# Layer 0 of a four-layer graph network: the last 20 nodes' softmax weights turned by TensorE, the first batch ahead of older values, and the output weights loaded from ScalarE's queue

## The chip, the cores and the metric

The kernel runs on one core of a Trainium2 chip. A core has five engines with a queue of instructions each: TensorE (PE; its weight loads are listed apart as PEld), VectorE (DVE), ScalarE (ACT), GpSimd (POOL) and SyncE (SP, which here issues transfers only). 16 DMA engines move the data. The metric is the device time of one execution in microseconds; the time of a kernel is the median over several runs.

## The reference

x is 2708 x 512, adj is 2708 x 2708, all f32. Four residual layers follow one another, each ended by a layer norm. The change touches the end of layer 0, which is attention over the graph with 8 heads of key width 64:

```python
keys = jnp.einsum('nj,hjk->hnk', node_matrix, Wks)
queries = jnp.einsum('nj,hjk->hnk', node_matrix, Wqs)
values = jnp.einsum('nj,hjk->hnk', node_matrix, Wvs)
atts = jnp.einsum('hqk,hmk->hqm', queries, keys) / key_dim ** 0.5
atts = atts - 1e+16 * (1.0 - adj)[None, :, :]
atts = jax.nn.softmax(atts, axis=-1)
return jnp.einsum('hqm,hmk,hko->qo', atts, values, Wo)
...
x = _layernorm(x + _L0_gnn_ref(x, adj, ...), axis=-1)
```

Layers 1 to 3 (a two-step linear layer with a normalised adjacency, a one-head graph attention, and a normalised graph convolution) come after it and are not touched.

## The kernel before

**Tiling.** The 2708 nodes are 22 chunks of 128 rows; the last, chunk 21 (`LAST`), has 20 rows. For queries, layer 0 works on items: one chunk and one pair of heads (j is the head in the pair, p the pair). There are 84 such items of class `Pair`, and one more of class `Last`, which packs all four pairs of the 20-row chunk into one item: query rows 32p to 32p+31 of its tiles belong to pair p, and of those the ones from `FILL` = 12 on are the 20 real ones.

**One item.** The nodes attended to are cut into three batches, chunks 0-7, 8-15 and 16-21 (`ends` = 0, 8, 16, 22; `ND` = 16).
- `scores` (L408): PE multiplies queries with keys into PSUM tiles pss (pool `ps_s`, tags s0 and s1 with two banks each); DVE adds the mask and keeps the row maximum (L421).
- `weights(k)` (L438): ACT takes the exponential of batch k in place, in tile s, and sums it (L443).
- The values need these weights with the attended nodes on the partitions, so each 128x128 block must be transposed. For the batches 0 and 1 that is done in two steps: `blocks` (L445) transposes blocks of 32x32 on DVE into a tile d (L450; one instruction of 128x1024 for each head), and `deal` (L455) moves groups of 32 partitions into a tile e with four transfers of 256 KB from SP's queue (L460).
- `turn` (L466): batch 2 is transposed on PE against the identity (L479 to L488, tiles pst), and ACT copies it out (L480, L489, L490; tiles pt, pt2, lastT).
- `values` (L514; for `Last` L555): PE sums V times the weights (L506) into av, for `Last` into four banks avz of `ps_s`, which take the order batch 2, 0, 1. At the end ACT copies av to ot (L526; `Last`: four copies into otz, L570), and POOL stores it in a DRAM tensor otd (L527, L571).

Pools: s 5 buffers, d 2, e 3, av 1.

**The loop.** Iteration i starts the scores of item i (`new`) while `cur` (item i-1) is turned into weights, and `late` and `old` (items i-2 and i-3) take their values. Under `manual_schedule` PE, DVE and ACT execute in the order in which the loop writes their instructions; SP's and POOL's order is made by the scheduler. In iteration 85 there is no new item: `cur` is the `Last` item, `late` the pair 3 of chunk 20, and `old` its pair 2, of which the values of nodes 8-15 are still to do. In iteration 86 `Last` takes its own values. Between, `heads_sums` (L575) reduces the row sums of the exponentials and takes reciprocals, and `heads_rows` (L588) transposes them on PE (prs), copies them on ACT (rst, L594) and stores them in DRAM as rs_d (L595, by POOL). `last_sums` (L597) does the same for the 20 rows (prz, rstz L605, rz_d L606). rst and rstz share one buffer.

**The po stage.** From L751 on, outside the manual order, each chunk c loads its heads from otd (otl, L753) and x (L754), loads the reciprocals broadcast over partitions (rb, L762, two transfers from rs_d, for the last chunk rz_d), multiplies on POOL (L763), multiplies with the output weights wo_sb on PE (po, L766, four matmuls a chunk), adds x on DVE (L767) and applies the layer norm. otl and rb have three buffers each. wo_sb (1 MB) is loaded ahead by `load_rows` (L112), which issues from SP at L113. The PSUM banks of po belong to a pool that is opened after the loop and takes over the banks of pst, av and the `ps_s` tiles.

Of the kernel before, what the change touches and what calls it, by code (L numbers as in the profile page):

```python
# [8 lines left out]
F32 = mybir.dt.float32  # L9
AF = mybir.ActivationFunctionType  # L10
# [5 lines left out]
P = 128  # L16
BLK = 512
# [5 lines left out]
def kernel(  # L23
# [22 lines left out]
    nc = tc.nc  # L46
# [11 lines left out]
    def cols(b):  # L58
        return b * BLK, min(BLK, N - b * BLK)
# [11 lines left out]
    ident = const.tile([P, P], F32, tag="ident", name="ident")  # L71
# [40 lines left out]
    def load_rows(t, src):  # L112
        nc.sync.dma_start(t, src.rearrange("(k p) f -> p k f", p=P))  # L113
# [3 lines left out]
    ends = [0, 8, 16, NC]  # L117
    ND = ends[2]
    KD4 = P // 32
# [16 lines left out]
    FILL = 32 - LR  # L136
    otd = [dram.tile([P, NP, rows(c)[1]], F32, tag=f"otd{c}", name=f"otd{c}") for c in range(NC)]
    with ExitStack() as l0:
# [12 lines left out]
        def batch(k):  # L151

            n0 = ends[k] * P
            return n0, min(ends[k + 1] * P, N) - n0
# [24 lines left out]
        def row_sums(c, k):  # L179

            r0, q = rows(c)
            a = loaded[c][0]
            n0, w = batch(k)
            dst = dgp[:, c, k : k + 1]
            if c == LAST:
                q, dst = 32, dgz[:, k : k + 1]
            nc.scalar.activation(a[:q, n0 : n0 + w], a[:q, n0 : n0 + w], AF.Copy, accum_out=dst[:q])  # L187
            if c == LAST and k == NW - 1:
                nc.sync.dma_start(dgp[:LR, c, :], dgz[FILL:32, :])
# [13 lines left out]
        def mask(c, k):  # L203

            n0, w = batch(k)
            a = loaded[c][0][:, n0 : n0 + w]
            nc.scalar.activation(a, a, AF.Identity, scale=1e16, bias=far)

        with tc.tile_pool(name="kvw", bufs=1) as kvw, tc.tile_pool(name="xTb", bufs=2) as xtp, tc.tile_pool(
            name="ps_0", bufs=8, space=PSUM  # L210
# [52 lines left out]
            for b in order:  # L263
                n0, w = cols(b)
# [108 lines left out]
        ps_s = l0.enter_context(tc.tile_pool(name="ps_s", bufs=2, space=PSUM, reuse_waits="tile"))  # L373
        sp = l0.enter_context(tc.tile_pool(name="sp", bufs=5, reuse_waits="tile"))
        dp = l0.enter_context(tc.tile_pool(name="dp", bufs=2, reuse_waits="tile"))
        ep = l0.enter_context(tc.tile_pool(name="ep", bufs=3, reuse_waits="tile"))
        ptp = l0.enter_context(tc.tile_pool(name="ptp", bufs=1, reuse_waits="tile"))

        class Pair:
# [58 lines left out]
            def weights(self, k):  # L438

                w = batch(k)[1]  # L440
                for j in range(2):
                    s = self.s[k][:, j, :w]
                    nc.scalar.activation(s, s, AF.Exp, bias=self.nm[j], accum_out=self.sums(j, k))  # L443

            def blocks(self, k, j):  # L445

                n = ends[k + 1] - ends[k]
                if k not in self.D:
                    self.D[k] = dp.tile([P, KD4, 2, n, 32], F32, tag="d", name=f"d{self.c}_{self.p}_{k}")
                nc.vector.transpose(  # L450
                    self.D[k][:, :, j].rearrange("p i m x -> p m i x"),
                    self.s[k][:, j, : n * P].rearrange("p (m i x) -> p m i x", i=KD4, x=32),
                )

            def deal(self, k):  # L455

                n = ends[k + 1] - ends[k]
                e = ep.tile([P, KD4, 2, n, 32], F32, tag="e", name=f"e{self.c}_{self.p}_{k}")
                for g in range(KD4):
                    nc.sync.dma_start(  # L460
                        e[:, g].rearrange("p j m x -> p (j m x)"),
                        self.D[k][32 * g : 32 * g + 32].rearrange("p i j m x -> p i (j m x)"),
                    )
                self.E[ends[k]] = e
# [30 lines left out]
            def weight(self, m, j):  # L495

                if m >= ND:
                    return self.pts[m, j]
                f = max(f for f in self.E if f <= m)
                return self.E[f][:, :, j, m - f, :]  # L500
# [28 lines left out]
        class Last(Pair):  # L529
# [19 lines left out]
            def weight(self, m, p, j):  # L549
                if m >= ND:  # L550
                    return self.pts[m, j][:, 32 * p + FILL : 32 * p + 32]
                f = max(f for f in self.E if f <= m)
                return self.E[f][:, p, j, m - f, FILL:]

            def values(self, m0, m1):  # L555
                if self.done == 0:
# [52 lines left out]
        items = [(c, p) for c in range(LAST) for p in range(NP)] + [(LAST, 0)]  # L609
        old = late = cur = None  # L610
        with tc.manual_schedule(
            engines={mybir.EngineType.PE, mybir.EngineType.DVE, mybir.EngineType.Activation}
        ):
            for i in range(len(items) + 3):
                new = None
                prep = i < len(items) and items[i][0] < LAST and items[i][1] > 0
                if cur is not None:
                    cur.weights(0)
                if i < len(items):
                    c, p = items[i]  # L620
                    if c + 1 < NC:
                        load_chunk(c + 1, p)
                    new = (Pair if c < LAST else Last)(c, p)
                    new.scores(0, 0)
                    new.scores(0, 1)
                if old is not None:
                    old.values(ends[1], ND)
                if prep:
                    row_sums(c + 1, p - 1)
                if cur is not None:  # L630
                    cur.weights(1)
                    cur.blocks(0, 0)
                    cur.blocks(0, 1)
                    cur.deal(0)
                if prep:
                    loops(c + 1, p - 1)
                if new is not None:
                    new.scores(1, 0)
                    new.scores(1, 1)
                if cur is not None:  # L640
                    cur.weights(2)
                if late is not None:
                    late.values(ND, NC)
                    late.values(0, ends[1])
                if cur is not None:
                    cur.blocks(1, 0)
                    cur.blocks(1, 1)
                    cur.deal(1)
                if prep:
                    mask(c + 1, p - 1)  # L650
                if new is not None:
                    new.scores(2, 0)
                    new.scores(2, 1)
                    new.maxima()
                if i in (HALF0 * NP + 2, len(items)):
                    sums = heads_sums(i == len(items))
                if cur is not None:
                    cur.turn()
                if i in (HALF0 * NP + 3, len(items) + 1):
                    heads_rows(*sums)  # L660
                if i == len(items) + 1:
                    last_sums()
                old, late, cur = late, cur, new
# [82 lines left out]

    with tc.tile_pool(name="wo", bufs=1, reuse_waits="tile") as wop:
        wo_sb = wop.tile([P, KC, D], F32, tag="wo", name="wo_sb")
        load_rows(wo_sb, wo)
        for c in range(NC):  # L750
            r0, q = rows(c)  # L751
            ot = wop.tile([P, NP, P], F32, tag="ot", name=f"otl{c}", bufs=3)
            nc.sync.dma_start(ot[:, :, :q], otd[c])  # L753
            nc.sync.dma_start(X[c][:q], x[r0 : r0 + q, :])  # L754
            rb = wop.tile([P, NP, P], F32, tag="rb", name=f"rb{c}", bufs=3)
            heads = rz_d if c == LAST else rs_d[c >= HALF0][c % HALF0]
            heads = heads.rearrange("j p q -> j (p q)")
            for j in range(2):
                dst = rb[j * KD : (j + 1) * KD]
                dst = dst[:, :, :q] if c == LAST else dst.rearrange("k p q -> k (p q)")  # L760
                src = rz_d[j, :, FILL:] if c == LAST else heads[j]
                nc.sync.dma_start(dst, src.partition_broadcast(KD))  # L762
            nc.gpsimd.tensor_tensor(ot[:, :, :q], ot[:, :, :q], rb[:, :, :q], ALU.mult)  # L763
            po = ps_acc.tile([P, BLK], F32, tag="acc", name=f"po{c}")
            for p in range(NP):
                nc.tensor.matmul(po[:q, :], ot[:, p, :q], wo_sb[:, p, :], start=(p == 0), stop=(p == NP - 1))  # L766
            nc.vector.tensor_tensor(X[c][:q], po[:q, :], X[c][:q], ALU.add)  # L767
            layernorm(X[c][:q], X[c][:q], q)
# [118 lines left out]
    if True:  # L887
# [115 lines left out]
        for b in range(NB):  # L1003
            for m, _ in enumerate(graph1(b)):
# [6 lines left out]
                if b == NB - 2 and m in (3, 7, 11, 15):  # L1011
                    c = first[(m - 3) // 4]
                    top0(c, 0, piece(c, 0))
                if b == NB - 1 and m < len(first):
                    c = first[m]
# [79 lines left out]
    if True:  # L1095
# [53 lines left out]
        for b in range(NB):  # L1149
            if b:  # L1150
                queue = Maxima(b + 1) if b + 1 < NB else None
            for m in graph2(b):
                if m % 4 == 2 and 0 <= m // 4 < len(chunks_of(b)) and b:
                    c = chunks_of(b)[m // 4]
# [25 lines left out]
    with tc.tile_pool(name="zp", bufs=2) as zp:  # L1180
# [87 lines left out]
        w = cols(TAIL)[1]  # L1268
# [22 lines left out]
        while n0 < NH * P:  # L1291
            w = min(BLK, NH * P - n0)
            n1 = NH * P + n0
            nchunks = w // P
            j = n0 // BLK
# [26 lines left out]
            m4, m7, e = banks(f"m4_{j}"), banks(f"m7_{j}"), banks(f"e0_{j}")  # L1322
# [13 lines left out]
            m3, m6, e = banks(f"m3_{j}"), banks(f"m6_{j}"), banks(f"e1_{j}")  # L1336
# [61 lines left out]
```

## Time and profile before

| | us |
|---|---|
| median of 3 runs | 2578.68 (2576.52 to 2579.57) |
| the profiled execution | 2579.97 |
| its span, from first to last instruction | 2578.2 |
| PE busy in it | 2515.9 |
| first scores' exponential of the `Last` item (L443) | starts 1216.91 |
| last values of the `Last` item on PE (L506) | end 1242.79 |
| first matmul of the po stage (L766) | starts 1245.40 |

The mean granted clock of PE over the span is 0.993 of full speed. In the profile each group of instructions is named by its line, engine and operation with the tiles that it writes and reads. An idle time in brackets is that of the engine before the instruction, with what ended it; "issue" there means that the profile shows nothing that was waited for. A wait for several things is put down to the one that came last. The engines' order around the change matters more than their totals: an instruction that waits holds up all that stands behind it in its engine's queue.

### The profile page before, as it was taken

How to read it: one execution, taken by the hardware profiler on the slowest of the kernel's cores; microseconds unless marked ns; L12 is line 12 of the kernel's file. 1: busy time of each engine (PE TensorE's matmuls, PEld its weight loads, DVE VectorE, ACT ScalarE, POOL GpSimd, SP SyncE). 2: the span in 40 equal slices, each digit the busy share in tenths (PEclk: the TensorE clock that was granted, in tenths of full speed). 3: DMA queues.
4: the chain of work that ended last, by engine and by line, in shares of the span. 5: the costliest groups of instructions: out<-in, count | busy, mean ns of one | idle time of the engine just before them, and what ended most of it. 6: DMA issues, size and time to landing. Idle time of an engine off the chain costs nothing.

```text
span 2578.2 us, 42561 instructions
## 1 busy us (share of the span) xinstructions
PE 2515.9 (98%) x15455; PEld 1501.4 (58%) x15455; DVE 1922.1 (75%) x4654; ACT 1212.3 (47%) x2418; POOL 312.4 (12%) x322
## 2 busy tenths in 40 slices
PE   9999999999999999999899999899999999999997
PEld 4775676767776767666556445444444465444465
DVE  2438999999999999998474777987776874543544
ACT  2114788788887887887011001565665640000000
POOL 1110000000000000000210000243332430000000
PEclk9999999999999999999899999999999999999999
DMA  5114888888888888888753444354433214644533
GB/s 175 66 33 120 235 209 212 231 215 219 229 207 236 213 214 235 213 215 193 217 182 99 126 121 140 120 157 135 125 113 112 64 31 115 184 141 143 178 102 107
DMA packets 221502, 411.45 MB, mean 160 GB/s; under 512 B 28766, under 2 KB 48912, under 8 KB 221293
## 3 DMA queue, kind: packets, MB, share of 16 engines
q1 hardware_dynamic: 215052, 392.00, 55.7%
q0 software_dynamic: 6240, 16.73, 1.7%
q8 instruction: 122, 2.00, 0.3%
q14 instruction: 88, 0.71, 0.1%
HBM read 213.55 MB, written 16.72 MB: 89 GB/s over the span
## 4 chain that ended last, share of the span: by engine, by line
PE 78%; issue 9%; DVE 7%; DMA 3%; ACT 1%; SPq 1%; POOL 0%; POOLq 0%; DVEq 0%; ACTq 0%
PE pss L399 15%; PE av L506 15%; PE acc L820 12%; PE acc L926 7%; PE m L1230 6%; PE psv L346 3%; PE pst L479 3%; PE pf L832 2%; PE po L766 2%; PE psk L242 2%; PE psq L242 2%; DMA e<-d 2%; PE ph L912 1%; DVE d L450 1%; DVE s L421 1%
## 5 line engine op out<-in xcount | busy, mean ns | idle before, releaser
L421 DVE CUSTOM_DVE_ANT_0 s<-pss,adj 128x512 f32<-128x512 f32 (+1 forms) x1020 | 574.3, 618 | 31.7 <-PE pss L399 30.0
L443 ACT ACTIVATE s<-s,nm 128x1024 f32<-128x1024 f32 (+1 forms) x510 | 527.7, 1037 | 18.7 <-DVE nm L436 17.2
L399 PE MATMUL pss<-KT,qt 64*128 64x512 f32 (+1 forms) x2016 | 459.8, 565 | 5.5 <-DVE mx L421 5.3
L450 DVE STREAM_TRANSPOSE d<-s 128x1024 f32<-128x1024 f32 x340 | 402.3, 1221 | 11.1 <-DMA e<-d 5.8
L820 PE MATMUL acc<-pt,x 128*128 128x512 f32 (+1 forms) x880 | 333.4, 537 | 12.4 <-ACT pt L873 9.7
L506 PEld LDWEIGHTS av<-e,V 128*64 128x64 f32 x5376 | 294.6, 137 | 62.7 <-DMA e<-d 47.8
L506 PE MATMUL av<-e,V 128*64 128x128 f32 x5376 | 326.3, 274 | 0.0
L399 PEld LDWEIGHTS pss<-KT,qt 64*128 64x128 f32 x2016 | 191.3, 186 | 142.3 <-issue 68.1
L820 PEld LDWEIGHTS acc<-pt,x 128*128 128x128 f32 x880 | 157.2, 191 | 188.2 <-issue 161.9
L926 PE MATMUL acc<-at,h 128*128 128x512 f32 (+1 forms) x504 | 196.8, 543 | 0.0
L884 POOL TENSOR_TENSOR cs<-cs,pt 128x512 f32<-128x512 f32 (+2 forms) x110 | 157.3, 1430 | 203.4 <-ACT pt L873 200.3
L871 DVE TENSOR_TENSOR pt<-pt,at 128x512 f32<-128x512 f32 (+2 forms) x132 | 107.6, 822 | 76.2 <-ACT pt L870 75.6
L527 POOL DMA_DIRECT2D otd<-ot x84 | 45.2, 538 | 969.1 <-ACT ot L526 956.7
L93 ACT ACTIVATE ln_t<-lnve 128x1 f32<-128x1 f32 x88 | 17.7, 201 | 307.8 <-DVE lnve L107 307.7
L1260 ACT ACTIVATE z<-pz,rdeg 128x512 f32<-128x512 f32 (+1 forms) x22 | 15.1, 688 | 311.7 <-PE pz L832 311.7
L926 PEld LDWEIGHTS acc<-at,h 128*128 128x128 f32 x504 | 90.2, 190 | 101.4 <-issue 99.2
L480 ACT COPY pt<-pst 128x512 f32<-128x512 f32 x170 | 91.4, 589 | 120.4 <-PE pst L479 120.2
L506 PEld LDWEIGHTS av<-pt,V 128*64 128x64 f32 x1680 | 90.0, 136 | 64.6 <-ACT adj L187 46.2
L873 ACT ACTIVATE pt<-pt 128x512 f32<-128x512 f32 (+2 forms) x132 | 76.1, 578 | 108.7 <-DVE pt L872 108.6
L937 DVE SCALAR_TENSOR_TENSOR cs<-at,rdeg,cs 128x512 f32<-128x512 f32 (+2 forms) x126 | 86.2, 684 | 43.5 <-DMA at<-in_adjT_dram 42.6
L506 PE MATMUL av<-pt,V 128*64 128x128 f32 x1680 | 110.3, 278 | 1.4 <-ACT ot L526 1.4
L783 ACT ACTIVATE at<-at,big 128x512 f32<-128x512 f32 (+2 forms) x132 | 83.5, 661 | 29.2 <-DMA at<-in_adjT_dram 29.2
(334 smaller groups left out, 3566.5 us busy)
## 6 DMA issues: line engine op xcount, KB each, us to landing
e<-d SPq DMA_DIRECT2D x680, 256.0 KB
at<-in_adjT_dram SPq DMA_DIRECT2D x210, 256.0 KB
a<-in_adj_dram SPq DMA_DIRECT2D x38, 677.0 KB
adj<-in_adj_dram SPq DMA_DIRECT2D x42, 512.0 KB
at_a<-in_adjT_dram SPq DMA_DIRECT2D x40, 256.0 KB
at_c<-in_adjT_dram SPq DMA_DIRECT2D x40, 256.0 KB
at_f<-in_adjT_dram SPq DMA_DIRECT2D x40, 256.0 KB
adj<-in_adj_dram SPq DMA_DIRECT2D x21, 330.0 KB
```

Of the source, the lines that this page charges most:

```text
L242: nc.tensor.matmul(ps[:, p, :], ws[i][:, k, p * P : (p + 1) * P], xs[i][:, k, :], start=(k == 0), stop=(k == FC - 1),)
L399: nc.tensor.matmul(pss[j][:, :w], qt[h, self.p, :], KT[h, self.p, n0 : n0 + w], start=True, stop=True)
L421: nc.vector.tensor_tensor_reduce(out=s[:, j, h0 : h0 + hw], in0=pss[j][:, :hw], in1=a[:, n0 + h0 : n0 + h0 + hw], scale=1.0, scalar=LOW, o ...
L443: nc.scalar.activation(s, s, AF.Exp, bias=self.nm[j], accum_out=self.sums(j, k))
L450: nc.vector.transpose(self.D[k][:, :, j].rearrange("p i m x -> p m i x"), self.s[k][:, j, : n * P].rearrange("p (m i x) -> p m i x", i=KD4 ...
L480: nc.scalar.copy(sb, pt)
L506: nc.tensor.matmul(self.av[j * KD : (j + 1) * KD, out], V[:, m, h * KD : (h + 1) * KD], weights[j], start=(self.done == 0), stop=(self.don ...
L820: nc.tensor.matmul(acc[k][:, :w], last[0][g : g + mr, :] if m == NC - 1 else values[:mr, k * P : (k + 1) * P], moving[g : g + mr, :w], sta ...
L871: nc.vector.tensor_tensor(pt[:mr, :w], pt[:mr, :w], at[:mr, :w], ALU.subtract)
L884: nc.gpsimd.tensor_tensor(sums[:mr, :w], sums[:mr, :w], pt[:mr, :w], ALU.add)
L926: nc.tensor.matmul(acc[hc][:, :w], lastH[g : g + mr, :] if m == NC - 1 else H[m][:mr, hc * P : (hc + 1) * P], at[g : g + mr, :w], start=(m ...
L1230: nc.tensor.matmul(acc[k][:, : moving.shape[1]], combined[which, m][:, k * P : (k + 1) * P], moving, start=(m == 0), stop=(stop and m == N ...
```

## The change

Three edits.

1. Class `Last` gets its own `weights`, `blocks` and `deal`. For batches 0 and 1 the exponential is written into a new tile dz of the d pool, with the columns of each block in another order: element (i, x) of a block, i of 4 and x of 32, goes to place 4x + i, so that consecutive results are written 16 bytes apart. `blocks` does nothing. `deal` transposes each 128x128 block of dz on PE into PSUM tiles psz (tags s0 and s1, four blocks a bank, 16 blocks a batch) and copies each bank on DVE into a tile ez of the e pool (four copies a batch). The four DVE transposes L450 and eight dealing transfers of this item are gone. `weight` reads the 20 columns of a pair from the new layout.
2. In iteration 85 (`end`) the values of nodes 8-15 of `old` are taken after `cur.deal(0)` rather than before ACT's `weights(1)`; on PE the 16 transposes of `Last`'s batch 0 stand ahead of them.
3. wo_sb is loaded by one transfer that ACT issues, with the same layout, in place of SP's L113. It stands at that place of ACT's order where the scheduler puts it: behind the copy lastT of the `Last` item and ahead of pair 3's ot.

```diff
                 f = max(f for f in self.E if f <= m)
-                return self.E[f][:, p, j, m - f, FILL:]
+                return self.E[f][:, j, m - f, 32 * p + FILL : 32 * p + 32]
+
+            def weights(self, k):
+
+                w = batch(k)[1]
+                n = ends[k + 1] - ends[k]
+                if ends[k] >= ND:
+                    return Pair.weights(self, k)
+                self.D[k] = dp.tile([P, 2, n, P], F32, tag="d", name=f"dz_{k}")
+                for j in range(2):
+                    nc.scalar.activation(
+                        self.D[k][:, j].rearrange("p m (x i) -> p m i x", i=KD4),
+                        self.s[k][:, j, :w].rearrange("p (m i x) -> p m i x", i=KD4, x=32),
+                        AF.Exp,
+                        bias=self.nm[j],
+                        accum_out=self.sums(j, k),
+                    )
+
+            def blocks(self, k, j):
+                pass
+
+            def deal(self, k):
+
+                n = ends[k + 1] - ends[k]
+                e = ep.tile([P, 2, n, P], F32, tag="e", name=f"ez_{k}")
+                for j in range(2):
+                    for m0 in range(0, n, 4):
+                        pt = ps_s.tile([P, BLK], F32, tag=f"s{j}", name=f"psz{k}_{j}_{m0}")
+                        for i in range(4):
+                            nc.tensor.transpose(pt[:, i * P : (i + 1) * P], self.D[k][:, j, m0 + i, :], ident)
+                        nc.vector.tensor_copy(e[:, j, m0 : m0 + 4, :], pt)
+                self.E[ends[k]] = e
...
-                if old is not None:
+                end = i == len(items)
+                if old is not None and not end:
                     old.values(ends[1], ND)
...
                     cur.deal(0)
+                    if end:
+                        old.values(ends[1], ND)
...
         wo_sb = wop.tile([P, KC, D], F32, tag="wo", name="wo_sb")
-        load_rows(wo_sb, wo)
+
+        nc.scalar.dma_start(wo_sb, wo.rearrange("(c p) n -> p c n", p=P))
```

## The prediction

> **What bounds the kernel now.** I read the page's busy shares first, then the stretches of the last batch of layer 0, then the timeline there. All times below are microseconds from the start of the span; L-numbers are lines of the kernel before.
>
> ```profile
> PE 2515.9 (98%) x15455; PEld 1501.4 (58%) x15455; DVE 1922.1 (75%) x4654; ACT 1212.3 (47%) x2418; POOL 312.4 (12%) x322
> ```
>
> TensorE (PE) is busy 98% of the span, so time is to be had only where it idles or runs at a lower clock. The change touches one place, 1216 to 1330. The columns of the stretches: bounds, length, busy time (and instructions) of PE, PE's weight loads, DVE, ACT and POOL, then granted clock, DMA share, GB/s.
>
> ```profile
> 1216.00:1220.00 4.00, 2.63 (x44) 2.25 (x44) 2.75 (x8) 4.00 (x10) 0.29 (x1) 1.00 0.93 211
> ...
> 1234.50:1237.90 3.40, 0.02 (x2) 0.00 (x0) 0.00 (x0) 0.00 (x0) 0.00 (x0) 0.93 0.86 254
> 1237.90:1242.80 4.90, 4.89 (x88) 4.77 (x87) 0.00 (x0) 0.56 (x4) 0.52 (x1) 0.50 1.02 265
> 1242.80:1245.40 2.60, 0.00 (x0) 0.00 (x0) 0.08 (x3) 0.17 (x1) 2.06 (x2) 0.50 0.96 235
> 1245.40:1251.00 5.60, 5.60 (x7) 2.50 (x8) 0.00 (x0) 0.00 (x0) 2.52 (x2) 0.50 0.07 25
> ```
>
> PE stands still for 1.4 at 1218, 3.4 at 1234.5 and 2.6 at 1242.8. From 1237.9 to 1251.0 the clock is half. The timeline says what was waited for (start, length, engine, line, operation, then in brackets the idle time before and what ended it):
>
> ```profile
> 1216.91 1.15 ACT L443 ACTIVATE s<-s,nm 128x1024 f32<-128x1024 f32 x1
> ...
> 1219.47 1.31 PE L506 MATMUL av<-pt,V 128*64 128x128 f32 x20 [1.37 <-ACT ot L526]
> ...
> 1222.87 2.37 DVE L450 STREAM_TRANSPOSE d<-s 128x1024 f32<-128x1024 f32 x2 [2.32 <-DMA e<-d]
> ...
> 1229.28 0.60 SPq L113 DMA_DIRECT2D wo_sb<-in_wo_dram  x1
> ...
> 1233.17 0.26 ACT L594 COPY rst<-prs 80x128 f32<-80x128 f32 x1 [6.46 <-PE prs L592]
> ...
> 1233.73 0.54 POOL L595 DMA_DIRECT2D rs_d<-rst  x1 [6.18 <-ACT rst L594]
> ...
> 1237.90 4.89 PE L506 MATMUL avz<-e,V 128*64 128x20 f32 x88 [3.38 <-issue]
> ...
> 1240.66 0.26 ACT L605 COPY rstz<-prz 2x128 f32<-2x128 f32 x1 [7.23 <-DMA rs_d<-rst]
> ...
> 1245.40 1.22 PE L766 MATMUL po<-wo_sb,otl 128*128 128x512 f32 x1 [2.61 <-POOL otl L763]
> ```
>
> What PE missed at 1234.5 is the dealt batch e_0_1: its four transfers are issued only after the transposes L450 at 1222.87, which had waited until 1222.65 for the buffer that pair 3's second deal (e_3_1) was leaving. The wait of ACT at 1240.66 (7.23 for the transfer rs_d) is hidden, because PE is late anyway. After 1245.4 comes the po stage: 22 chunks of 3.43 on PE and at least 3.37 on DVE, so one engine follows the other. Its first seven matmuls ran at half clock: DVE's first addition stands at 1251.98, 6.58 after po's start instead of 3.43, a loss of 3.15. At its far end PE waits 1.31 and 1.68 for copies behind DVE's last chunks, which lag PE by 4.1.
>
> **The change part by part.** I work out when DVE's first addition of the po stage starts.
>
> *Removed:* four L450 of 1.19 on DVE, and eight 256 KB transfers with their issues on SP. With them PE's 3.38 idle goes. POOL's multiply of the first loaded tile no longer stands behind the transfers rz_d and otd (1241.21, 1243.29), so the 2.61 before po goes too.
>
> *Added:* 32 PE transposes and 8 DVE copies out of PSUM. The trace has 8 such transposes (L479) in 1.09 to 1.39, so 16 cost 2.2 to 2.8; I take 2.4. PSUM copies of 512 columns on DVE take 0.68. The eight copies (5.4) lie in DVE's idle time: those of the first batch end by about 1228 and are read at 1237.4, those of the second by about 1232 and are read at 1241.6, so 9 of cover in each.
>
> *The new wait on ACT.* The exponentials of the last item now write a dealing buffer. The first may start when the deals of e_3_0 have landed: between 1216.91 (ACT's start before) and 1218.1 (DVE used that buffer at 1218.18). Before, a pair took 2.27 until ACT was free for its next instruction (1216.91 to 1219.18), so it ends by 1220.4; the last 8 transposes (1.2) and pair 2's 1.97 of moved matmuls end by 1223.6. The second pair of exponentials needs e_3_1 landed, 1222.65, and leaves ACT free at 1222.70 + 2.27 = 1224.97. Queued behind them on ACT is the copy ot of pair 2, for which PE's pair-3 values wait; from its start to theirs it was 0.29 before. They start at 1225.26, where before they started at 1219.47: 5.8 late, the price of the change.
>
> *PE from there:* pair 3's first values 3.21 (1.31 + the rest to 1222.7), transposes 2.4, the older transposes 1.72, pair 3's last values 1.9, the last item's own 2.85, first batch 3.9, prs and prz 0.34, second batch 3.9. So prs is done at 1241.6 and the second batch at 1245.5, at full clock (before: 1242.8).
>
> *What is late next.* rs_d hangs on prs. Before, the issue of rs_d lay 0.56 after the copy rst began, so now it is at 1242.15. ACT's rstz waits for its landing, since both use one buffer; behind rstz stand four otz copies of 0.17, and po needs a bank that the last of them frees. The two landings in the trace:
>
> ```profile
> DMA to landing us min/median/max: 4.6/5.7/6.8
> ```
>
> With 1.0 for rstz, otz and the steps between, po starts at 1243.15 + 4.6, 5.7 or 6.8: 1247.75, 1248.85, 1249.95. DVE's first addition stands 3.43 later at full clock: 1251.2, 1252.3 or 1253.4 against 1251.98, so -0.8, +0.3 or +1.4. I take the middle, +0.3: fewer transfers run beside it than before, but SP's x loads then come.
>
> *The clock.* PE idles 2.2 to 4.4 before po. The trace has shown both answers: no drop after 1.4 at 1218, a drop after 3.38 at 1237. It costs 0 to 3.15. The middle gap, 3.35, is as long as the one that dropped it; but there the drop came at 1237.3, 2.8 into the gap, and only part of a later gap need fall so. I take 0, at little better than even chances. The Trainium skill ("TensorE: Matmul & The Clock Gate", The HAM clock gate) speaks of a free-running window of about 3.4 us after which an idle PE goes to half rate; the 3.38 gap agrees, and by that rule the middle case would be on the edge, with up to the price just named on top.
>
> *The strided write.* The exponential now writes f32 at steps of 16 bytes; no ACT row shows that. Lower bound: free. The nearest row is POOL's copy L341, which reads at steps of 128 bytes for chunks below ND (the group at 101) and in unbroken runs for those above (the group at 176.9):
>
> ```profile
> 101.08 4.14 POOL L341 COPY xp<-xb 128x512 f32<-128x512 f32 x4 [11.39 <-issue]
> ...
> 176.89 2.28 POOL L341 COPY xp<-xb 128x512 f32<-128x512 f32 x4 [11.39 <-issue]
> ```
>
> The four copies of the one group start 1.02 apart and took 1.08 each; those of the other took 0.62: 1.75 times. On ACT that would be 0.86 for each exponential, and the two of the second batch lie on the path: +1.7. I take 0, as this row is another engine and a read, and keep +1.7 for the range. The Trainium skill ("SBUF — State Buffer", Door 1: the note on cachelines) says that each access to a new 16-byte line pays unless a line is hit at least twice, which these writes never do; it names no price.
>
> *wo_sb by ACT.* It is issued behind the copy lastT, at about 1233.1 (before 1229.28), and landed 9.9 after issue before; so 1243.0 at worst, under the 4.7 before po's start. SP's second rb2 load waits for it and x_0 to x_4 are behind it; x_0 is wanted at 1252. No cost; with that cover gone po would wait for it one for one.
>
> *The far end.* If DVE's lag of 4.1 shrinks, up to 3.0 of PE's waits go (1.31 + 1.68); if it grows, some 1 more. I take 0.
>
> **Sum:** +0.3 on the profiled execution's 2579.97 (span 2578.2 and 1.8 around it). That execution lies 1.29 above the median 2578.68, so I add to the median: 2579.0.
>
> **Rivals.**
> *It gains.* For it: the work of PE alone from 1216.13 adds up to 24.6, so with no new wait po could start 4.7 sooner than before. Say the wait for e_3_1 did not decide: the second pair of exponentials then leaves ACT at 1221.5, and pair 2's matmuls end at 1222.4, so that pair 3's start at 1222.7, 2.6 sooner; with a landing of 4.6, po at 1245.15, DVE at 1248.6, -3.4; with PE's 3.0 at the far end gone too, -6.4: 2572.3. Against: those transfers land at 1222.65 with little else on the DMA at the time.
> *The clock falls (slower).* PE's gap before po reaches 3.4 and more, as at 1234.5: at 6.8 of landing, +1.4 + 3.15 = +4.55. PE also has only some 4.4 of work (2.4 + 1.97) between 1216.1 and 1225.3; half clock over a stretch of 3.4 behind it loses 1.7 more: +6.25, 2584.9. It decides once an idle stretch passes about 2.8, as from 1234.5 to the drop at 1237.3.
> *The strided write costs.* At POOL's ratio +2.0 in all, 2580.7; past 0.2% only from some 3.1 times the contiguous time (0.3 + 2 x 1.14 x 2.15 = 5.2).
> *The order is not what the text says:* the order of PE, DVE and ACT is fixed as written, so I give it nothing.
>
> **How the numbers follow.** 0.2% is 5.2 us, about what a measurement of this kernel can tell from no change. The forecast (within that) gets 0.47, including the strided write at POOL's price; gain beyond it 0.20; the clock 0.22 and a strided write of 3.1 times or more 0.11 make slower, 0.33. The likeliest case alone spans 2574.9 (-0.8 and -3.0 at the far end) to 2582.8 (+1.4, strided 1.7, far end 1.0). The range goes on to both rivals, and past the slower one by the strided write's 1.7: 2572.3 to 2586.6.
>
> **What would show it.** In the profile after: the second pair of exponentials should start near 1222.7 behind a wait for DMA e<-d, and each last 1.14; PE's pair-3 values should wait for ot until about 1225.3; rstz should wait for rs_d until about 1248; po should start behind otz, not behind POOL. Wrong if the exponentials last twice as long, if the stretch 1216 to 1226 or that before po shows a clock of 0.5, or if po waits for wo_sb.

## The result, and the profile after

| | before | changed |
|---|---|---|
| median of 18 runs, us | 2578.06 (2570.62 to 2587.08) | 2586.48 (2580.3 to 2594.4) |
| ratio, with its 95% interval | | 1.0032 (1.0022 to 1.0042) |
| profiled execution, us | 2579.97 | 2583.58 |
| its span, us | 2578.2 | 2581.8 |

The changed kernel is slower by 0.32%, some 8.3 us (5.7 to 10.8). That is past the 0.2% within which the forecast expected it, and 0.1 us below the upper end of the stated range.

The timeline of the changed kernel around the change (start, length, engine, line, operation; in brackets the idle time before, and what ended it):

```profile
1218.96 2.09 ACT L563 ACTIVATE dz<-s,nm 128x1024 f32<-128x1024 f32 x1 [0.49 <-DMA e<-d]
...
1224.51 2.15 ACT L563 ACTIVATE dz<-s,nm 128x1024 f32<-128x1024 f32 x1 [1.46 <-DMA e<-d]
...
1225.24 17.31 SPq L797 DMA_DIRECT2D rb<-rs_d  x4
...
1228.48 0.25 ACT L526 COPY ot<-av 128x128 f32<-128x128 f32 x1
...
1228.78 1.31 PE L506 MATMUL av<-pt,V 128*64 128x128 f32 x20 [1.88 <-ACT ot L526]
...
1235.40 0.41 ACTq L784 DMA_DIRECT2D wo_sb<-in_wo_dram  x1
...
1242.65 2.43 SPq L789 DMA_DIRECT2D x<-in_x_dram  x5
...
1244.49 0.58 POOL L626 DMA_DIRECT2D rs_d<-rst  x1 [4.88 <-ACT rst L625]
...
1249.81 0.26 ACT L636 COPY rstz<-prz 2x128 f32<-2x128 f32 x1 [5.61 <-DMA rs_d<-rst]
...
1250.43 11.78 PE L801 MATMUL po<-wo_sb,otl 128*128 128x512 f32 x21 [2.58 <-issue]
...
1256.72 0.69 DVE L802 TENSOR_TENSOR x<-po,x 128x512 f32<-128x512 f32 x1 [8.72 <-issue]
```

Four things are to be seen. The exponential that writes at steps takes 2.09 to 2.15 us instead of 1.15, and as both of the second batch stand in front of the copy ot, PE's pair-3 values wait until 1228.78. SP stops in the middle of the rb loads at 1225.24 and goes on at 1240.8, when wo_sb, issued by ACT only at 1235.40, has landed: in the trace that landing, at 1240.81, releases the next rb load. Then five x loads leave at once, 1242.65 to 1245.1, and the small transfer rs_d, issued among them at 1244.49, lands 5.2 later. And po begins behind that.

The stretches of the changed kernel (columns as before: bounds, length, PE, PE's loads, DVE, ACT, POOL, clock, DMA share, GB/s):

```profile
1221.00:1225.00 4.00, 3.65 (x18) 2.99 (x20) 0.00 (x0) 2.54 (x5) 0.00 (x0) 0.57 0.93 275
...
1248.00:1250.40 2.40, 0.00 (x0) 0.01 (x1) 0.00 (x1) 0.52 (x5) 0.05 (x1) 0.64 0.22 82
1250.40:1255.60 5.20, 5.17 (x6) 2.18 (x7) 0.00 (x0) 0.00 (x0) 2.57 (x3) 0.51 0.09 11
```

The clock (the column after POOL's) falls twice, at 1221 and in the gap before po, and po's first six matmuls run at half of it. Finally the second half of the po stage. Before, PE hardly waits there for POOL's multiply:

```profile
PEld po L766 <- POOL otl L763: 1.9, 3, 1.4
...
PE po L766 <- POOL otl L763: 0.6, 1, 0.6
```

After, it does, chunk by chunk, and POOL itself waits there for rb, which it does not before (total, times, longest; the same waits from some 1290 on):

```profile
POOL otl L798 <- DMA rb<-rs_d: 10.9, 3, 4.5
PEld po L801 <- POOL otl L798: 10.6, 10, 2.3
...
PE po L801 <- POOL otl L798: 3.6, 4, 1.5
```

One scale is used for all kernels below, since the start of this part drifts by some us from execution to execution: the distance from the end of pair 3's transposes on PE (line L488 before; 1216.21 before, 1217.67 after). It is worked out from the starts and ends in each timeline. "Layer 1" is the start of the ninth matmul of layer 1's first product (ph), which waits for a copy that stands behind the po stage on DVE.

| kernel (edits in it) | pair 3's values | po | first addition | first to last addition | layer 1 | ratio to before (95%) |
|---|---|---|---|---|---|---|
| before | 3.3 | 29.2 | 35.8 | 77.9 | 116.2 | |
| before, again | 3.3 | 28.3 | 34.1 | 77.4 | 114.1 | 0.9999 (0.9986 to 1.0013) |
| changed (1, 2, 3) | 11.1 | 32.8 | 39.1 | 79.7 | 121.8 | 1.0032 (1.0022 to 1.0042) |
| 3 alone | 3.3 | 30.3 | 35.9 | 76.3 | 114.8 | 0.9991 (0.9980 to 1.0001) |
| 3 alone, again | 3.3 | 30.1 | 36.7 | 77.4 | 116.7 | 0.9997 (0.9986 to 1.0008) |
| 1, 2 | 11.6 | 31.0 | 34.7 | 77.3 | 114.6 | 1.0003 (0.9993 to 1.0012) |
| 1, 3 | 6.8 | 29.9 | 35.5 | 79.7 | 118.3 | 1.0017 (1.0006 to 1.0028) |
| 1 alone | 6.8 | 26.6 | 30.4 | 77.7 | 110.7 | 1.0005 (0.9996 to 1.0014) |
| changed, own rstz buffer | 11.6 | 31.0 | 34.8 | 80.8 | 119.3 | 1.0007 (0.9997 to 1.0017) |
| changed, dz in s pool | 9.5 | 31.6 | 37.0 | 79.9 | 120.0 | 1.0023 (1.0013 to 1.0034) |
| changed, reads at steps | 11.0 | 33.5 | 39.3 | 81.7 | 124.6 | one run |
| changed, SP in written order | 11.7 | 37.0 | 43.6 | 79.5 | 125.8 | 1.0054 (1.0035 to 1.0073) |
| 1, 2, dz in s, own rstz | 10.1 | 29.5 | 34.9 | 76.0 | 113.0 | 1.0007 (0.9995 to 1.0019) |
| 1, dz in s, own rstz | 5.9 | 25.3 | 29.1 | 75.7 | 106.8 | 0.9993 (0.9984 to 1.0002) |

### The profile page after: what moved, and what is told of

Its sections match the earlier page's. It is cut to its first block, busy times and chain, and to the rows that moved or that the text cites. A ratio compares the mean times of both kernels' runs of the same rounds, so it can differ in the third digit from the quotient of the medians.

```text
span 2581.8 us, 42620 instructions
## 1 busy us (share of the span) xinstructions
PE 2518.8 (98%) x15487; PEld 1504.6 (58%) x15487; DVE 1922.5 (74%) x4658; ACT 1215.5 (47%) x2418; POOL 312.3 (12%) x322
## 5 line engine op out<-in xcount | busy, mean ns | idle before, releaser
L450 DVE STREAM_TRANSPOSE d<-s 128x1024 f32<-128x1024 f32 x336 | 397.6, 1222 | 6.9 <-DMA e<-d 5.8
```

Of the source, the lines that this page charges most:

```text
L450: nc.vector.transpose(self.D[k][:, :, j].rearrange("p i m x -> p m i x"), self.s[k][:, j, : n * P].rearrange("p (m i x) -> p m i x", i=KD4 ...
```

## The experiments

**The load of wo_sb alone.** Edit 3 put into the kernel before.

```diff
-        load_rows(wo_sb, wo)
+        nc.scalar.dma_start(wo_sb, wo.rearrange("(c p) n -> p c n", p=P))
```

> The kernel before with only the output weights' load moved from SP to ACT. Theory 'SP order': the longer po stage of the changed kernel (DVE's first addition to its last: 79.66 us against 77.86 before) comes from the order in which the loads now stand on SP; here SP's order changes too, but the next layer's weight loads stay closer to their old place, so 78 to 79.7, and 0 to +2 us against the kernel before. Theory 'all of the loss lies in the turned item': no change of the time, first addition within 1 us of its old distance from the end of pair 3's transposes (35.9 us).

The ratio was 0.9991 and the stage 76.3: the SP theory missed, as the stage became shorter, not longer. The other came as it said, with no change of the time and the first addition at 35.9, but the next experiment speaks against it. Here ACT issues the load at 1224.3, when its queue is free, not at 1235.4, and no load of SP waits for its landing at 1233.9. It was timed and profiled a second time, since the interval left open whether it gains:

> The kernel before with the output weights' load issued by ACT, timed again: 0.9991 of the time before, interval 0.998 to 1.0001, leaves it open whether that edit gains when it stands alone. Theory 'a shorter po stage gains': again 1 to 4 us faster, stage 76 to 77.5. Rival 'a chance of one profile': equal, stage 77 to 79.

0.9997, stage 77.4, as the rival said. By itself the edit does nothing that can be measured, or gains a little; no loss shows (the upper ends of the intervals are 1.0001 and 1.0008).

**The change without it.** Edits 1 and 2, wo_sb by SP.

```diff
-        nc.scalar.dma_start(wo_sb, wo.rearrange("(c p) n -> p c n", p=P))
+        load_rows(wo_sb, wo)
```

> The changed kernel with the output weights loaded by SP as before. Theory 'SP order': the po stage is back at 77.9 us from first to last addition and the kernel about 2 us faster than the changed one, still 5 to 6 us slower than before, since the strided exponentials (2.1 us instead of 1.15) and the wait for rs_d remain and the first addition stays 39 us behind the end of pair 3's transposes. Theory 'all in the turned item': as slow as the changed kernel, stage 79.7.

1.0003: as fast as before, some 7.5 us better than the changed kernel, more than the 2 us expected. The stage is back at 77.3, as the SP theory said, and PE's waits for POOL in its second half are gone (0.3). But the first addition came back too, from 39.1 to 34.7, which it did not say. The timeline of this kernel tells why:

```profile
1217.69 0.82 SPq L113 DMA_DIRECT2D wo_sb<-in_wo_dram  x1
...
1226.78 2.91 SPq L789 DMA_DIRECT2D x<-in_x_dram  x3
...
1242.43 0.54 POOL L626 DMA_DIRECT2D rs_d<-rst  x1 [6.18 <-ACT rst L625]
...
1244.31 0.25 ACT L636 COPY rstz<-prz 2x128 f32<-2x128 f32 x1 [2.17 <-DMA rs_d<-rst]
...
1246.12 10.11 PE L801 MATMUL po<-wo_sb,otl 128*128 128x512 f32 x23 [0.32 <-issue]
```

wo_sb and the first x loads are long over when rs_d is issued, and it lands in 1.8 instead of 5.2. It is then done before PE's last values, po starts without a gap (0.32), and the clock stays at 1.00. The strided exponentials are the same 2.1 in both kernels. The other traces agree on rs_d: it lands in 1.8 to 2.5 in the four with edit 1 and not 3, in 4.3 to 6.3 in the six with both.

**A buffer for rstz.** The changed kernel; rstz no longer waits for rs_d.

```diff
-            rst = small.tile([P, P], F32, tag="rst", name="rstz", bufs=1)
+            rst = small.tile([P, P], F32, tag="rstz", name="rstz", bufs=1)
```

> The changed kernel with a buffer of its own for rstz, so that it does not wait for the transfer rs_d. Theory 'rs_d and the clock': PE's gap before po falls from 2.6 to under 1 us, the clock stays at 1.00 there, the first po chunk takes 3.4 instead of 6.2 us, and the first addition comes 34.6 us (39.1 - 1.7 - 2.8) behind the end of pair 3's transposes; the kernel gains about 4.5 us on the changed one. Rival 'the strided exponential is the whole of it': the gap and the clock do not matter, first addition stays at 38 to 39.

As the first theory said: first addition 34.8 (34.6 expected), gap 0.32, clock 1.00 at po. The ratio 1.0007 is 6.4 us better than the changed kernel. The stage stays long, 80.8: that part of the loss is another one.

**dz in the pool of s.** The changed kernel; the exponentials need not wait for the dealing transfers.

```diff
-                self.D[k] = dp.tile([P, 2, n, P], F32, tag="d", name=f"dz_{k}")
+                dz = sp.tile([P, 2, SW], F32, tag="s", name=f"dz_{k}")
+                self.D[k] = dz.rearrange("p j (m q) -> p j m q", q=P)
```

> The changed kernel with the dz tiles in the pool of the score tiles s, whose old contents are used up, so that the exponentials do not wait for the dealing transfers. Theory 'the wait for e<-d is on the path': the second pair of exponentials starts about 4.3 us behind the first rather than 5.6, both earlier by the waits of 0.5 and 1.5 us; PE's pair-3 values start about 1.9 us sooner, first addition 37.2 instead of 39.1 us behind the end of pair 3's transposes (if the clock before po does as in the changed kernel), 2 us gained. Rival: the strided writes alone set ACT's pace, nothing gained.

Pair 3's values start 1.6 sooner, the first addition 2.0 sooner (37.0), the ratio is 1.0023, some 2 us better, though the two intervals overlap. The waits of 0.5 and 1.5 were on the path.

**The permutation on the reading side.** The changed kernel, s read at steps of 128 bytes, dz written in one run.

```diff
-                        self.D[k][:, j].rearrange("p m (x i) -> p m i x", i=KD4),
-                        self.s[k][:, j, :w].rearrange("p (m i x) -> p m i x", i=KD4, x=32),
+                        self.D[k][:, j].rearrange("p m (x i) -> p m x i", i=KD4),
+                        self.s[k][:, j, :w].rearrange("p (m i x) -> p m x i", i=KD4, x=32),
```

> The changed kernel with the permutation on the other side of the exponential: s is read at steps of 128 bytes and dz is written in one run. Theory 'a write at 16-byte steps pays, a read does not': an exponential of 128x1024 takes 1.15 us again and pair 3's values start some 1.9 us sooner. Theory 'each access to a new place pays on either side': 2.1 us or more, nothing gained.

```profile
1218.84 2.05 ACT L563 ACTIVATE dz<-s,nm 128x1024 f32<-128x1024 f32 x1 [0.80 <-DMA e<-d]
```

2.05 to 2.09: the price is nearly the same on either side, so the first theory is out and the second fits. It was one run without repetition, and its time is not used.

**Pair 2's values first.** The changed kernel without edit 2.

```diff
-                if old is not None and not end:
+                if old is not None:
...
-                    if end:
-                        old.values(ends[1], ND)
```

> The changed kernel without its second edit: pair 2's values go ahead of the turned first batch again. Theory 'the order costs': ot of pair 2 no longer stands behind the second pair of exponentials, pair 3's values start 6 instead of 11 us behind the end of pair 3's transposes, the last item's values end some 3 us sooner, first addition about 36 instead of 39 us, and the kernel is about 3 us faster than the changed one. Rival 'the order gains, as the transposes fill PE': pair 3's values no sooner, kernel 1 to 2 us slower than the changed one.

By the trace the order costs: pair 3's values at 6.8 (6 expected), first addition 35.5 (36). The times agree, 1.0017 against 1.0032, though the two intervals overlap. rs_d still lands slowly (6.2) among the x loads, and the stage is still 79.7.

**SP in written order.** The changed kernel, with `tc.manual_schedule(engines={mybir.EngineType.SP})` around the loop of the po stage.

> The changed kernel with the loads of the po stage in written order on SP (otl, x, rb of one chunk, then the next; the next layer's loads go where they fit). Theory 'SP order': the po stage takes 77 to 78.2 us from first to last addition instead of 79.7, PE no longer starts chunks right behind POOL's multiply in its second half, and some 2 us are gained on the changed kernel. Rival 'the stage is long from collisions on DVE and POOL': 79 to 80, nothing gained.

A miss: 79.5, and slower than the changed kernel. In this order loads of layer 1 come behind the first otl load, and SP stands before them, 14.9 us until PE has done its transposes at 1234.97 and 3.1 more until 1239.52. The first x load leaves at 1240.00 and the first rb load at 1240.60, before wo_sb lands at 1241.52. po starts at 37.0, and rb of a chunk is issued last of its three loads; POOL waits for rb even longer than in the changed kernel (24.8 instead of 10.9 from 1290 on). So this kernel does not test the theory. What the others show is that the stage is long where edits 1 and 3 stand together: 79.7 to 81.7 in the five traces with both and the scheduler's order, 75.7 to 77.9 in the other eight. From 1290 to 1332 PE's weight loads wait 9.3 to 11.5 for POOL in the five, at most 2.6 in the eight, and POOL waits 4.5 to 15.0 for rb in the five, at most 3.3 in the eight. That it is the order on SP which makes rb late is argued from this, not shown, and which place in the order decides was not tried.

**Edits 1 and 2 with all three mends.** wo_sb by SP, dz in s, own rstz.

> The turned item with wo_sb loaded by SP, dz in the s pool and a buffer of its own for rstz. If the losses named so far are all there is: pair 3's values start about 9.5 us behind the end of pair 3's transposes, po starts without a gap over 0.5 us at a clock of 1.00, first addition 33.5 to 34.5 us (before 35.8), stage 77.3 to 78, and the kernel is 0 to 3 us faster than before. Rival: the gain is taken back in the po stage, where DVE is as long as PE, and the kernel equals the one before.

By the trace nearly as expected: pair 3's values at 10.1, no gap before po (0.32), stage 76.0 and layer 1 at 113.0, but the clock was half in po's first chunk, so that the first addition came at 34.9. The clock fell at 1247.08 although PE had been busy for 3.23 of the 3.41 us before, so a gap before po is not all that can bring it down; what else does stays open. By the time it was the rival: 1.0007.

**Edit 1 alone, and with the mends.** Pair 2's values first, wo_sb by SP; then also dz in s and an own rstz.

> The first edit alone: the last item turned by TensorE, pair 2's values first, wo_sb loaded by SP. Theory 'the turn gains, the other two edits lose more': pair 3's values start 6 us behind the end of pair 3's transposes, the last item's values end some 26.5 us behind it, rs_d lands in 2 to 4 us and po starts at 27 to 28 (before 29.2) at a clock of 1.00 or nearly, first addition 30.5 to 33 (before 35.8), stage 77 to 78; 3 to 5 us faster than before. Rival 'the strided exponentials and the transposes cost what the transfers did': first addition 35 to 36, as fast as before.

> The first edit alone with dz in the s pool and a buffer of its own for rstz. Theory: with pair 2's values first, neither the wait for e<-d nor that for rs_d is on the path any more, so within 1 us of the first edit alone in the first addition (30.5 to 33) and 3 to 6 us faster than before. Rival: rstz still holds up po there, and this one is 1 to 3 us faster than the first edit alone.

By the traces the first theory, and a little more: pair 3's values at 6.8 and 5.9, po at 26.6 and 25.3, both at full clock from 1216 on until the first addition at 30.4 and 29.1. The stretches of edit 1 alone:

```profile
1216.00:1222.00 6.00, 3.26 (x43) 2.72 (x42) 2.13 (x8) 5.13 (x8) 0.00 (x0) 1.00 0.88 211
1222.00:1226.00 4.00, 4.00 (x64) 3.75 (x63) 1.29 (x2) 3.16 (x3) 0.54 (x1) 1.00 0.89 289
1226.00:1242.40 16.40, 16.32 (x418) 15.23 (x414) 3.63 (x8) 5.46 (x16) 2.91 (x4) 1.00 0.53 149
1242.40:1246.50 4.10, 3.78 (x10) 1.82 (x10) 0.08 (x4) 0.17 (x1) 3.25 (x3) 1.00 0.11 14
```

PE is busy all but 3 us of 30, and layer 1 starts 5.5 and 9.4 sooner than in the first trace of before. But the times do not follow: 1.0005 (0.9996 to 1.0014) and 0.9993 (0.9984 to 1.0002), where 3 to 5 and 3 to 6 us were expected. The second is the fastest version with the turned item, and its interval still holds 1; its first addition is 1.3 sooner than the first's, a little more than the 1 expected. Between edit 1 alone and edits 1 and 2 (1.0003) the times show nothing either, so a cost of edit 2 shows in the times only where edit 3 is made, though the traces show it in both places (first addition 34.7 against 30.4 without edit 3).

**Before, again.**

> The kernel before, profiled and timed again, as a scale for what one profile is worth. Theory 'the profiled execution before was a slow one around the change': the clock is not half from 1237.9 to 1251 here, first addition 31 to 34 us behind the end of pair 3's transposes instead of 35.8, which would explain why the kernels with the turned item gain 3 to 6 us more in their traces than in their times. Rival 'the trace before is typical': first addition within 1 us of 35.8, the half clock there again, and the rest is given back in the later layers. The ratio should be 1 within its interval.

The ratio is 1 within its interval. Neither expectation fits the trace: the first addition came at 34.1, and the clock was half here too, from 1239.6 to 1249.8. The waits differ:

```profile
1234.50:1237.90 3.40, 3.40 (x119) 3.40 (x119) 0.00 (x0) 0.22 (x1) 0.54 (x1) 1.00 0.98 258
1237.90:1242.80 4.90, 0.48 (x18) 0.38 (x14) 0.08 (x3) 0.16 (x1) 0.00 (x0) 0.67 1.03 311
1242.80:1245.40 2.60, 0.00 (x0) 0.00 (x0) 0.00 (x0) 0.37 (x5) 2.21 (x3) 0.50 0.91 272
...
1245.84 10.37 PE L766 MATMUL po<-wo_sb,otl 128*128 128x512 f32 x19 [7.46 <-POOL otl L763]
```

This time the dealt batch came in time, PE ran through at full clock and then waited 7.46 for POOL, where before it had waited 3.38 and 2.61. So the same kernel's layer 1 starts at 116.2 or 114.1: a trace tells which waits that execution had, and what they are worth only to a few us. That takes some 2 us off what the traces seemed to promise for edit 1, not all of it. Layers 1 to 3 vary by more than that, with half-clock stretches that come and go from one execution to the next (below): from the start of layer 1 to the end it is 1248.1 and 1250.1 us in the two versions with edit 1, 1245.8 and 1251.6 in the two traces of before. Against the first trace of before that takes back 2.3 and 4.3, against the second nothing. Whether edit 1 loses there on the average of all executions was not settled, so where its gain went in the times stays open.

## Why the prediction came out as it did

The steps by the common scale, predicted and measured:

| step | predicted | measured |
|---|---|---|
| an exponential of the turned item | 1.14 (bound 2.0) | 2.09 to 2.15 |
| pair 3's values start | 9.05 | 11.1 |
| landing of rs_d | 5.7 (4.6 to 6.8) | 5.2 |
| gap before po | 3.35 | 2.6 |
| po starts | 32.6 | 32.8 |
| first po chunk until the addition | 3.43 (bound 6.58) | 6.29 |
| first addition | 36.1 | 39.1 |
| first to last addition | 77.9 (-3 to +1) | 79.7 |

**Right:** which waits there would be. The exponentials behind e<-d, the copy ot behind them, rstz behind rs_d, po behind otz and not behind POOL, and the 8 copies hidden: all stand in the timeline. po's start came within 0.2, though by luck, as two errors went against each other: ACT was 2.1 later, and PE then needed 19.1 instead of 20.2 and waited 0.8 less.

**Wrong in size, strided write.** "I take 0, as this row is another engine and a read". The row told the price: the exponentials of the second batch start 2.00 apart instead of 1.14, which makes the +1.7 that was kept for the range. That is most of the 2.1 by which pair 3's values came late against the prediction; 0.35 is the later landing of e<-d.

**Wrong in choice, clock.** "I take 0, at little better than even chances." It fell 0.8 into the gap of 2.6, where the prediction's scale was a drop 2.8 into a gap of 3.38. It cost 2.5 (6.29 against 3.76 in the kernel with edits 1 and 2, at full clock; the 3.43 left out 0.3 between PE and DVE). In the second trace of before it fell as well.

**Wrong in its place, wo_sb by ACT.** "No cost" looked only at po's wait for wo_sb, and there it was right. The prediction named SP's rb2 and the x loads behind it, and counted on the x loads beside rs_d, for which it took the middle landing: 5.7, and 5.2 came. But it took that landing from the rows of before, which hid that edit 3 brings it: with edits 1 and 2 alone it is 1.8. And together with edit 1 the same edit lengthens the stage by some 2, where the prediction took 0 for the far end and up to 1 as a loss. Edit 3 undone brings the time back to 1.0003, so most of the 8.3 us goes with this edit, but only on top of edit 1: alone it issues wo_sb 9 us sooner by the common scale and costs nothing. A buffer of its own for rstz brings back nearly as much (1.0007), so by the times the larger part runs through the wait for rs_d.

**The case that came** is the slower one named "the clock falls", with its price of 6.25 between the 5.6 and 7.7 by which layer 1 starts later than in the two traces of before, though made up otherwise: against the first, 3.3 until the first addition and 2.3 in and behind the stage. The rival with the strided write was part of it. Of the gain rival nothing showed. That the time still lies inside the range is partly luck: the range had room for the clock and the strided write, not for the longer stage.

## What to carry to other kernels

Before a load is moved to another queue, find out when that queue comes to it, and which transfers of the old queue wait for it: a stopped queue lets go all at once, and then small transfers that something waits for stand among big ones. A permutation taken into an instruction is not free because the instruction is needed anyway; look for any row that pays for steps, on whatever engine. And a kernel that gains 5 us at one place in one trace has not gained them until it is timed: here the traces named the waits and the times took back most of the sum.

## What the runs showed of the hardware

ACT's exponential of 128x1024 f32 took 2.09 us writing at steps of 16 bytes, 2.05 reading at steps of 128 bytes, and 1.15 with neither. The Trainium skill ("SBUF — State Buffer", the note on cachelines under Door 1) says that each access that crosses to a new 16-byte line pays a penalty, and names no price; these runs agree, on reads and writes of ACT alike. No run tries a step under 16 bytes, so the length of the line is not shown here.

The half-clock stretches of an execution all start on one grid of 3.413 us, throughout its 2578 us. The remainder of their starts divided by 3.413 was 1.76 in the first trace of before, 0.52 in the second, 2.83 in the changed kernel, and between 0.18 and 3.23 in the fourteen traces. In layers 1 to 3 they come mostly at the same few places of the program, but 1 to 7 steps of the grid long in all, by execution: 3 and 7 in the two traces of before, 1 in the changed kernel, 5 and 6 in edit 1 alone and with the mends. These layers are the same in all kernels. A straight line through the fourteen traces gives 1239.6 us from the start of layer 1 to the end, and 1.64 for each step at half clock (correlation 0.95, the farthest trace 2.2 off the line). The Trainium skill ("TensorE: Matmul & The Clock Gate", The HAM clock gate) tells of a free-running window of about 3.4 us, which agrees. These layers alone took from 1242.3 to 1251.6 us, a spread of 9.3, more than the whole effect that was looked for.
